# Attention and gated MLP in fp32 on one core: output weights of the last group in another place, matrix transposes for two block pairs instead of four, another order

## The chip, the cores and the metric

The kernel runs on one core of a Trainium2 chip. Its time is the device time of one execution in microseconds (us). TensorE is called PE here, VectorE DVE, ScalarE ACT, GpSimd POOL; SP is the engine whose queue issues nearly all DMAs.

## The reference

Two batches of 512 tokens with 512 features go through one post-normalised block, all in fp32:

```python
q, k, v = x @ Wq.T, x @ Wk.T, x @ Wv.T            # 32 query heads, 8 key/value heads of 128
q, k = rmsnorm(q) * q_norm_w, rmsnorm(k) * k_norm_w
scores = q @ k.T / sqrt(128) + slope[head] * (key_pos - query_pos)   # causal
x = layernorm(x + softmax(scores) @ v @ Wo.T)
h = silu((x @ gate.T) * gate_s) * ((x @ up.T) * up_s)                # int32 weights, 1376 wide
out = layernorm(x + (h @ down.T) * down_s)
```

## The kernel before

**Tiling.** A group is one key/value head with its four query heads; there are eight. A unit is a group, a batch and a block of 128 tokens, `(g, b, i)`; 64 units. Units go in pairs of neighbouring blocks, numbered 0 to 31: groups 0 to 5 for both batches each, then groups 6 and 7 for batch 0, then 6 and 7 for batch 1. Pair 0 is `(0, 0, 0..1)`, pair 1 is `(0, 0, 2..3)`, pairs 30 and 31 are `(7, 1, 0..1)` and `(7, 1, 2..3)`.

**Seven products.** Most matrix products are done as seven block products in place of eight (`seven`, `PLAN`). They need sums and differences of blocks of both factors, which DVE and POOL make ahead, partly in place: `sums_x` for the tokens (`sx`, and `xT` itself, one half of a batch at a time), `sums_q` for a group's q, k and v weights (`tq`), `sums_o` for its output weights (`to`). `project` does q, k and v of a pair so, except for pair 0, which `project_plain` does directly. Each product has a PSUM bank, named `pa`, `pb` or `pc`, which ACT or DVE empties into `c`. For groups 0 to 5 `project_out` applies the scheme twice, one inside the other, and needs a second level of sums, `ti`; for groups 6 and 7 (`g >= DEEP`) `project_pair` uses one level and no `ti`.

**A pair's way.** `heads` squares and sums q and k, takes the inverse root (a power on POOL, `inv`), scales into `sq`, and turns it so that features lie on partitions (`qT`, and `kT` with the key weights `kw`). There are two ways to turn a block. One: `nc.tensor.transpose` on PE into PSUM (`ptq`, `ptk`) and copies out. The other: DVE transposes squares of 32 x 32 (L1152), the result is written to DRAM in one DMA (`far_q`) and read back in another order (`qT<-far_q`), and ACT and POOL weigh the keys. `scores` multiplies by the keys (`sc`), adds the bias and takes the maximum on DVE, the exponential on ACT, and scales by the inverse sums. `attend` turns each 128 x 128 block of the result the same two ways: `pt` on PE, or DVE squares (`st`), a DMA to `far` and two DMAs back to `prT`. It then multiplies by the values (`pa` at L1370, `px` and `pz` at L1402). Which way a block goes is set by

```python
NEAR_Q = {(0, 0), (HKV - 1, 1)}
NEAR_P = {(0, 0), (HKV - 1, 1)}
```

as group and batch: pairs 0, 1, 30 and 31 use PE. The two ways leave the keys of a block in different orders, so the values of those pairs are put in the other order by DMA (`v`, `vs`), and the norm weights are kept in both orders (two columns of `qw` and `kw`).

**Output weights.** `load_o` brings a group's 1 MB into `wo`. There is one such buffer, so a load waits until the last product of the group before has read it. Groups 6 and 7 alternate, and each is loaded twice.

**Order.** Every piece of work is an entry of `Work` with a cost on each engine that may do it, a priority and its dependences. `Work.order` places the entries one after the other, always the one that can start first by these costs, and so picks engines, buffers and the order in each queue. A DMA counts there as its start plus 1.6, its size, and 0.6. `SHIFTS` is a list of seeds; each moves the priorities of the entries in a stretch at random before the order is made. On the chip each engine works through its own list in order and waits for semaphores.

**After the attention.** `norm1` normalises and transposes (`ptx`), `ffn_up` and `ffn_down` do the MLP.

Of the kernel before, what the change touches and what calls it, by code (L numbers as in the profile page):

```python
# [14 lines left out]
ALU = mybir.AluOpType  # L15
# [25 lines left out]
MAX_INIT = 3e38  # L41
NEAR_Q = {(0, 0), (HKV - 1, 1)}
NEAR_P = {(0, 0), (HKV - 1, 1)}
DEEP = HKV - 2
# [27 lines left out]
def pool_ts(n):  # L72
# [5 lines left out]
SHIFTS = (  # L78
    1000003, 1000006, 1000008, 1000014, 1000017, 1000025, 1000044, 1000058, 1000062, 1000075,
    1000109, 1000133, 1000283, 1000470, 1000520,  # L80
)
# [49 lines left out]
class Buf:  # L131


    def __init__(self, ring, name):
        self.ring, self.name = ring, name
        self.users = []
        self.home = None
        self.tile = None

    def make(self):  # L140
        ring, k = self.home
        self.tile = ring.pool.tile(
            ring.shape, ring.dtype, tag=f"{ring.name}{k}", name=self.name, bufs=1
        )

    def __getitem__(self, i):
# [3 lines left out]
class Work:  # L150
# [68 lines left out]
    def order(self):  # L219
# [43 lines left out]
        while ready:  # L263
            at_engine = {}
            for o in ready:
                t0 = room(o)
                if t0 is None:
                    continue
                for e, c in o["costs"].items():
                    s = max(t0, free.get("ACT" if e == "ACTQ" else e, 0.0))  # L270
                    if e == "POOL":
                        s = max(s, port["DVE"])
                    elif e == "DVE" and o["port"]:
                        s = max(s, port["POOL"])
                    at_engine.setdefault(e, []).append((s, o["prio"], s + c, o["n"], c))
            assert at_engine, "no work can start: " + ", ".join(
                b.name for o in ready for b in o["takes"]
            )
            best = None
            for e, found in at_engine.items():  # L280
                first = min(found)
                if best is None or first < best[0]:
                    best = (first, e)
            (s, _, _, n, c), e = best
            o = ops[n]
            ready.remove(o)
            if e == "ACT" and o["table"] and o["table"] != table[0]:
                table[0] = o["table"]
                c += TABLE
            o["eng"] = e  # L290
            if e in ("SP", "ACTQ"):
                free["ACT" if e == "ACTQ" else e] = s + o["issue"]
                dma = max(dma, s + 1.6) + c
                o["end"] = dma + 0.6
            elif e == "NONE":
                o["end"] = s
            else:
                free[e] = s + c
                o["end"] = s + c
                if e == "POOL" or (e == "DVE" and o["port"]):  # L300
                    port[e] = s + c
            o["start"] = s
            for b in o["takes"]:
                if b.home is None:
                    b.ring.take(b)
            for r in o["opens"]:
                r.open = True
            placed.append(o)
            for x in nexts[o["n"]]:
                left[x["n"]] -= 1  # L310
                if not left[x["n"]]:
                    x["at"] = at(x)
                    ready.append(x)
# [26 lines left out]
def post_ln_block(  # L340
# [53 lines left out]
    r_us = ring("all", "us", 1, [P, NF])  # L394
    r_qw = ring("all", "qw", 1, [P, 2])
    r_kw = ring("all", "kw", 1, [P, HKV + 1, 2])
    r_id = ring("all", "ident", 1, [P, P])
# [19 lines left out]
    r_kT = ring("att", "kT", 2, [P, S])  # L417
    r_v = ring("att", "v", 2, [P, NTB, HD])
    r_qT = ring("att", "qT", 2, [P, 2, NQ, (G + 1) * Q])
# [41 lines left out]

    w_qkv, w_o = {}, {}

# [52 lines left out]
    def load_o(g, prio):  # L516
        wo = Buf(r_wo, f"wo_{g}")
        w_o[g] = wo
        load(1.05, prio, lambda q: q.dma_start(wo.tile, wot[g]), [(wo, m) for m in range(4)])

# [249 lines left out]

    t_q, t_o, t_i = {}, {}, {}

    def sums_q(g, prio):
# [10 lines left out]
        )  # L784

    def sums_o(g, prio, after):

        t, w = Buf(r_to, f"to_{g}"), w_o[g]
        t_o[g] = t
        block = {(0, 1): 0, (0, 0): 1, (1, 1): 2, (1, 0): 3}  # L790
# [7 lines left out]
            after=after,  # L798
        )
        if g >= DEEP:  # L800
            return
# [14 lines left out]

    c_of, qTs, kTs, vs, v2s, prTs, aTs = {}, {}, {}, {}, {}, {}, {}

# [10 lines left out]
    def project_plain(p, prio):  # L829
# [5 lines left out]
        for (r, n), rg in zip([(0, 0), (0, 1), (1, 0), (1, 1)], (r_f, r_f, r_f, r_po)):  # L835
            banks[r, n] = Buf(rg, f"pp_{r}_{n}")
        for kc in range(NK):
# [122 lines left out]
    def heads(p, prio):  # L960
# [4 lines left out]
        if i == 0:  # L965
            kTs[g, b] = Buf(r_kT, f"kT_{g}_{b}")
            vs[g, b] = Buf(r_v, f"v_{g}_{b}")
        kT, v = kTs[g, b], vs[g, b]
        sq = Buf(r_sq, f"sq_{p}")
# [59 lines left out]
        for r in range(2):  # L1029

            def normed(e, r=r):
                if e == "ACT":
                    for h in range(G + 1):
                        nc.scalar.activation(  # L1034
                            sq[:, r, h, :],
                            c(r)[:, ts(h, HD)],
                            AF.Copy,
                            scale=inv[:, r, h : h + 1],
                        )
                    return  # L1040
                vec[e].tensor_tensor(
                    sq[:, r],
                    c(r)[:, : 5 * HD].rearrange("p (h d) -> p h d", h=G + 1),
                    inv[:, r].unsqueeze(2).to_broadcast([P, G + 1, HD]),
                    ALU.mult,
                )

# [8 lines left out]


        v2 = Buf(r_vs, f"vs_{p}")
        v2s[p] = v2
        if (g, b) in NEAR_P:  # L1060
            for m in range(NQ):
# [3 lines left out]
                    prio + 0.2,  # L1065
                    lambda q, m=m, at=at: q.dma_start(
                        v[ts(m, Q), i : i + 2, :], cb[at : at + H2 - 1 : 2, :, 1, 2 * HD :]
                    ),
                    [(v, (i + r, m)) for r in range(2)],
                    [(cb, (r, 1)) for r in range(2)],  # L1070
                )
            for m in range(2):
                load(
# [8 lines left out]
        else:  # L1082
            for r in range(2):
                copy_op(
                    HD,
                    prio + 0.2,
                    lambda r=r: v[:, i + r, :],
                    lambda r=r: c(r)[:, 5 * HD :],
                    [(cb, (r, 1))],
                    [(v, (i + r, m)) for m in range(NQ)],  # L1090
                    ("ACT", "POOL"),
                )
            copy_op(
# [6 lines left out]
                ("ACT", "POOL"),  # L1100
            )
        qT = qTs[p] = Buf(r_qT, f"qT_{p}")
        if (g, b) in NEAR_Q:
            for r in range(2):
# [23 lines left out]
            def evict_k(e):  # L1128
                dst = kT[:, i * P : (i + 2) * P].rearrange("p (m k r) -> p m k r", m=4, k=2)
                src = ptk[:, : 2 * P].rearrange("p (m r k) -> p m k r", m=4, k=2)  # L1130
                if e == "ACT":
                    nc.scalar.activation(dst, src, AF.Copy, scale=kw[:, g, 1:2])
                else:
                    nc.vector.tensor_scalar_mul(dst, src, kw[:, g, 1:2])

# [48 lines left out]
        for x in range(2):  # L1184

            def weigh(e, x=x):
                dst = kT[:, i * P : (i + 2) * P].rearrange("p (m k x c) -> p x m k c", k=2, x=2, c=Q // 2)
                src = qT[:, :, :, G * Q :].rearrange("p r (m x) (c k) -> p x (r m) k c", x=2, k=2)
                if e == "ACT":
                    nc.scalar.activation(dst[:, x], src[:, x], AF.Copy, scale=kw[:, g, 0:1])  # L1190
                else:
                    nc.gpsimd.tensor_scalar(
                        dst[:, x], src[:, x], kw[:, g, 0:1], 1.0, ALU.mult, ALU.mult
                    )
# [103 lines left out]
    def attend(u, prio):  # L1298
# [6 lines left out]
        key = f"{g}_{b}_{i}"  # L1305
        pr, v = pr_of[i], vs[g, b]
        p, r = divmod(units.index(u), 2)
        for j in range(i + 1):
            prT = prTs[u, j] = Buf(r_prT, f"prT_{key}_{j}")
# [5 lines left out]
            n = (NQ - a0) * Q  # L1315
            if (g, b) in NEAR_P:
                pt = Buf(r_po, f"pt_{key}_{j}")
# [80 lines left out]
        def halves(e):  # L1398
            for m, (q, j) in enumerate(both):
                prT = prTs[(g, b, j), j]  # L1400
                for k, (bank, val) in enumerate(zip(banks, (v[:, j, :], v2s[q].tile))):
                    nc.tensor.matmul(  # L1402
# [10 lines left out]
        for q, j in both:  # L1413
            reads += [(prTs[(g, b, j), j], m) for m in range(2)]
            reads += [(v, (j, m)) for m in range(NQ)] + [(v2s[q], m) for m in range(2)]
        W.add({"PE": 1.07}, prio + 0.4, halves, reads, [A(bank) for bank in banks])
# [358 lines left out]
    for p in range(NP):  # L1775
# [3 lines left out]
        if p > 0 and fresh:  # L1779
            load_qkv(g, u - 14.0)  # L1780
            load_o(g, u - 10.0)
        if p == 0:
            project_plain(p, u - 2.4)
        if fresh:
            sums_q(g, u - 3.0)
        if p > 0:
            if g == 0 or (g == 1 and b == 0 and i == 0):
                sums_x(b, i // 2, u - 3.0, lead if p > 1 else ())
            project(p, u - 2.4)
        heads(p, u - 1.8)  # L1790
# [412 lines left out]
```

## Time and profile before

| | |
|---|---|
| median of 3 runs | 970.32 us (969.92 to 971.77) |
| profiled execution | 973.81 us, its span 972.0 |
| granted PE clock, mean | 0.994 |
| PE busy | 98% of the span |
| DVE, POOL, ACT busy | 74%, 55%, 50% |
| DMA, mean | 152 GB/s, 147.71 MB in all |
| first matmul, end of the last | 1.3 us, 966.2 us after the span's start |

The profile is one execution. An instruction's row gives start and length; lengths of matrix instructions overlap, so the next may start before the one before has ended. An fp32 product of two 128-row tiles shows as two rows. Idle time stands with the instruction that came after it and with what ended it. The granted clock is the share of full speed that PE was given.

### The profile page before, as it was taken

The page shows a single profiled execution, that of the slowest core. Times are in us where ns is not written, and L with a number is a line of the kernel's source. Part 1 is how long each engine was busy: PE and PEld are TensorE (multiplying, and loading weights), DVE is VectorE, ACT ScalarE, POOL GpSimd, SP SyncE. Part 2 cuts the span into 40 slices and gives each one's busy share as a digit, 9 for nine tenths or more (in the row PEclk, how much of TensorE's full clock was granted, in tenths as well). Part 3 has the DMA queues.
Part 4 walks back from the last instruction along what each step waited for, and adds up shares of the span by engine and source line. Part 5 has one row for each costly group of instructions (what it writes and reads, how often), then busy time and mean ns, then how long its engine had stood idle before and what let it go on. Part 6 is the DMA issues. An engine that isn't in the chain of part 4 may idle for free.

```text
span 972.0 us, 14179 instructions
## 1 busy us (share of the span) xinstructions
PE 955.3 (98%) x4330; PEld 692.5 (71%) x4330; DVE 716.8 (74%) x1765; ACT 487.5 (50%) x1342; POOL 531.6 (55%) x592
## 2 busy tenths in 40 slices
PE   8999999999999999999999999999899999999997
PEld 5666766676767675766677666676677888888886
DVE  7666877878887878887777888776575666667644
ACT  2576475656555646556545656755354333333000
POOL 5666365659565837665777865967453432132120
PEclk9999999999999999999999999999899999999999
DMA  9133567756674847684746775865431233210001
GB/s 324 37 112 106 154 211 235 206 175 197 178 217 134 252 122 232 194 244 158 204 158 193 232 221 162 233 195 168 141 123 65 68 96 87 82 52 23 23 23 44
DMA packets 182797, 147.71 MB, mean 152 GB/s; under 512 B 26208, under 2 KB 166368, under 8 KB 181440
## 3 DMA queue, kind: packets, MB, share of 16 engines
q1 hardware_dynamic: 181856, 146.13, 49.2%
q8 instruction: 35, 0.57, 0.2%
q10 hardware_dynamic: 864, 0.66, 0.2%
q14 instruction: 42, 0.34, 0.1%
HBM read 92.62 MB, written 53.48 MB: 150 GB/s over the span
## 4 chain that ended last, share of the span: by engine, by line
PE 95%; DMA 3%; DVE 1%; SPq 0%; POOL 0%; issue 0%; POOLq 0%; DVEq 0%
PE pa_q L725 16%; PE sc L1227 12%; PE pa L1370 11%; PE pb_q L725 8%; PE pa_h L725 8%; PE pa_o L1594 8%; PE pb_h L725 4%; PE pb_o L1594 4%; PE pc_q L725 4%; PE pa_d L725 4%; PE pa_o L725 3%; PE pc_h L725 2%; PE pc_o L1594 2%; PE pb_d L725 2%; DMA wo<-in_wot_dram 2%; PE px L1402 2%
## 5 line engine op out<-in xcount | busy, mean ns | idle before, releaser
L1252 ACT ACTIVATE pr<-pr,nmax 128x48 f32<-128x48 f32 (+15 forms) x256 | 133.5, 522 | 97.3 <-DVE nmax L1236 95.8
L1227 PE MATMUL sc<-kT,qT 128*128 128x48 f32 (+15 forms) x512 | 153.3, 408 | 0.0
L1236 DVE CUSTOM_DVE_ANT_0 pr<-sc,bias 128x48 f32<-128x48 f32 (+15 forms) x256 | 110.2, 441 | 36.4 <-PE sc L1227 33.2
L1370 PE MATMUL pa<-prT,v 128*128 128x512 f32 (+1 forms) x320 | 135.9, 510 | 0.5 <-DMA prT<-far 0.4
L1227 PEld LDWEIGHTS sc<-kT,qT 128*128 128x128 f32 x512 | 86.9, 191 | 42.1 <-issue 19.2
L666 DVE TENSOR_TENSOR acc<-acc,pa_o 128x512 f32<-128x512 f32 (+2 forms) x128 | 72.7, 568 | 49.6 <-PE pa_o L1594 25.1
L1284 ACT ACTIVATE pr<-pr,rden 128x64 f32<-128x64 f32 (+12 forms) x213 | 92.3, 495 | 16.1 <-DVE rden L1267 15.9
L725 PE MATMUL pa_q<-tq,sx 128*128 128x384 f32 x248 | 90.2, 487 | 0.0
L942 DVE STREAM_TRANSPOSE st<-pr 128x512 f32<-128x512 f32 (+1 forms) x140 | 84.0, 634 | 2.4 <-POOL pr L1286 1.3
L652 POOL TENSOR_TENSOR inv<-ms,nhalf 128x10 f32<-128x10 f32 (+1 forms) x33 | 65.7, 1992 | 22.1 <-DVE ms L1014 20.8
L1370 PEld LDWEIGHTS pa<-prT,v 128*128 128x128 f32 x320 | 55.3, 191 | 22.3 <-issue 5.0
L822 ACT COPY gu<-pa_h 128x256 f32<-128x256 f32 (+1 forms) x88 | 32.1, 370 | 77.5 <-PE pa_h L725 63.3
L725 PEld LDWEIGHTS pa_q<-tq,sx 128*128 128x128 f32 x248 | 46.0, 190 | 29.9 <-issue 7.5
L822 ACT COPY c<-pa_q 128x384 f32<-128x384 f32 x78 | 37.1, 476 | 57.8 <-PE pa_q L725 49.0
L977 ACT ACTIVATE sq<-c 128x640 f32<-128x640 f32 x64 | 45.2, 730 | 32.0 <-DVE c L1152 23.4
L1034 ACT ACTIVATE sq<-c,inv 128x128 f32<-128x128 f32 x160 | 50.1, 389 | 14.6 <-POOL inv L652 14.6
L1286 POOL TENSOR_SCALAR pr<-pr,rden 128x64 f32<-128x64 f32 (+10 forms) x75 | 34.8, 475 | 37.4 <-DVE rden L1267 37.2
L666 POOL TENSOR_TENSOR si<-so 128x384 f32<-128x384 f32 x21 | 21.0, 1001 | 59.1 <-PE pb_o L1594 57.1
L1000 DVE TENSOR_REDUCE ms<-sq 128x5 f32<-128x640 f32 x64 | 51.1, 811 | 0.5 <-ACT sq L977 0.5
L1152 DVE STREAM_TRANSPOSE c<-sq 128x320 f32<-128x320 f32 x112 | 50.7, 485 | 0.0
L1594 PEld LDWEIGHTS pa_o<-ti,si 128*128 128x128 f32 x336 | 42.9, 192 | 8.1 <-issue 2.9
L1252 ACT ACTIVATION_READ_ACCUMULATOR pr<-pr,nmax 128x1 f32 x256 | 48.0, 188 | 0.0
(238 smaller groups left out, 2242.7 us busy)
## 6 DMA issues: line engine op xcount, KB each, us to landing
far<-st SPq DMA_DIRECT2D x112, 256.0 KB, 2.9
prT<-far SPq DMA_DIRECT2D x224, 128.0 KB, 3.1
far_q<-c SPq DMA_DIRECT2D x28, 640.0 KB, 3.8
qT<-far_q SPq DMA_DIRECT2D x56, 320.0 KB, 3.8
w<-in_wqkv_dram SPq DMA_DIRECT2D x39, 384.0 KB, 4.9
wo<-in_wot_dram SPq DMA_DIRECT2D x10, 1024.0 KB, 7.1
far<-st SPq DMA_DIRECT2D x28, 128.0 KB, 2.5
prT<-far SPq DMA_DIRECT2D x56, 64.0 KB, 2.8
```

Source lines behind the costliest of these rows:

```text
L652: lambda e: nc.gpsimd.tensor_tensor(dst(), src(), nhalf[:, :n], ALU.pow),
L666: lambda e: vec[e].tensor_tensor(dst(), a(), b(), alu),
L725: nc.tensor.matmul(bank[:rows, :width], lhsT=a(fa, c), rhs=b(fb, c), start=(fresh and c == 0), stop=(c == depth - 1), skip_group_check=True,)
L822: nc.scalar.copy(dst(), src())
L942: {"DVE": dve(n)}, prio, lambda e: nc.vector.transpose(dst(), src()), reads, [A(st)]
L1000: lambda e, r=r: nc.vector.tensor_reduce(ms[:, r], sq[:, r], AX.X, ALU.add),
L1227: lambda e, a=a, w=w, sc=sc: nc.tensor.matmul(sc[:, :w], lhsT=qT[:, r, a, : G * Q], rhs=kT[:, :w], start=True, stop=True),
L1236: lambda e, a=a, w=w, sc=sc: nc.vector.tensor_tensor_reduce(out=pr[:, a, :w], in0=sc[:, :w], in1=bias[:, S - w :], scale=-(SHRINK**-g), sc ...
L1252: lambda e, a=a, w=w: nc.scalar.activation(pr[:, a, :w], pr[:, a, :w], AF.Exp, bias=nmax[:, a : a + 1], scale=-1.0, accum_out=den[:, a : a ...
L1284: nc.scalar.activation(dst, src, AF.Copy, scale=rden[:, a : a + 1])
L1370: lambda e, j=j, prT=prT, n=n: nc.tensor.matmul(by_head(po.tile)[:, :, P - n // G :], lhsT=v[:, j, :], rhs=late(prT, j, n), start=(j == 0) ...
L1594: nc.tensor.matmul(bank[:, ts(c, P)], lhsT=a(fa, c), rhs=b(fb, c), start=fresh and c == 0, stop=True, skip_group_check=True,)
```

## The change

1. `load_o` for the last group takes its buffer from the ring of `ti` (seen through `view` in the shape of `wo`), after everything that used `ti` for groups 0 to 5. Group 6 keeps the buffer of `wo`. The first step of each `sums_o` also waits for the last of the one before.
2. `NEAR = {0, 31}` replaces the two sets: pairs 0 and 31 alone turn blocks on PE. Pairs 1 and 30 go by DRAM. For the near pairs the normalisation writes the features in the order that the other way gives, so `qw` and `kw` keep one column. A pair's values are kept in the order that each later pair of its group and batch will need: in `vn` by DMA, in `v` by copies, or in both (for pairs 0 and 30). The ring of `v` has three buffers.
3. A DMA's start counts as 2.0 in the planner, and there are other seeds. The order changes throughout.

```diff
-NEAR_Q = {(0, 0), (HKV - 1, 1)}
-NEAR_P = {(0, 0), (HKV - 1, 1)}
+NEAR = {0, 31}
+PLAIN = 1
...
 SHIFTS = (
-    1000003, 1000006, 1000008, 1000014, 1000017, 1000025, 1000044, 1000058, 1000062, 1000075,
-    1000109, 1000133, 1000283, 1000470, 1000520,
+    22000003, 22000016, 22000019, 22000030, 22000031, 22000059, 22000062, 22000085, 22000096,
+    22000110, 22000180, 22000208, 22000219, 22000282, 22000333, 22000351, 22000369, 22000431,
+    22000607, 22000642,
 )
...
-                dma = max(dma, s + 1.6) + c
+                dma = max(dma, s + 2.0) + c
...
-    r_v = ring("att", "v", 2, [P, NTB, HD])
+    r_v = ring("att", "v", 3, [P, NTB, HD])
...
     def load_o(g, prio):
-        wo = Buf(r_wo, f"wo_{g}")
+        if g == HKV - 1:
+
+            flat = lambda t: t.rearrange("p j n c -> p (j n c)")[:, : 4 * DM]
+            view = lambda t: flat(t).rearrange("p (m k c) -> p m k c", m=4, k=2)
+            wo = Buf(r_ti, f"wo_{g}", view)
+            after = [o for t in t_i.values() for o in t.users]
+        else:
+            after = []
+            wo = Buf(r_wo, f"wo_{g}")
         w_o[g] = wo
-        load(1.05, prio, lambda q: q.dma_start(wo.tile, wot[g]), [(wo, m) for m in range(4)])
+        load(1.05, prio, lambda q: q.dma_start(wo[:, :], wot[g]), [(wo, m) for m in range(4)], after=after)
...
         t, w = Buf(r_to, f"to_{g}"), w_o[g]
+
+        after = after + [last_sums[-1]] if last_sums else after
...
             def normed(e, r=r):
+                dst = sq[:, r]
+                src = c(r)[:, : 5 * HD].rearrange("p (h d) -> p h d", h=G + 1)
+                if p in NEAR:
+                    dst = dst.rearrange("p h (r m) -> p h m r", m=NQ)
+                    src = src.rearrange("p h (m r) -> p h m r", m=NQ)
...
-        if (g, b) in NEAR_P:
+        users = [q for q in range(NP) if pairs[q][:2] == (g, b) and pairs[q][2] >= i]
+        if any(q in NEAR for q in users):
+            if (g, b) not in vns:
+                vns[g, b] = Buf(r_v, f"vn_{g}_{b}")
+            vn = vns[g, b]
...
+        if any(q not in NEAR for q in users):
+            if (g, b) not in vs:
+                vs[g, b] = Buf(r_v, f"v_{g}_{b}")
+            v = vs[g, b]
...
-        if (g, b) in NEAR_Q:
+        if p in NEAR:
...
-            if (g, b) in NEAR_P:
+            if p in NEAR:
...
-        if p == 0:
+        if p < PLAIN:
             project_plain(p, u - 2.4)
```

## The prediction

> **What bounds the kernel now.** I read the page first: one engine is busy nearly throughout.
>
> ```profile
> PE 955.3 (98%) x4330; PEld 692.5 (71%) x4330; DVE 716.8 (74%) x1765; ACT 487.5 (50%) x1342; POOL 531.6 (55%) x592
> ```
>
> So a microsecond counts if it is TensorE (PE) work or a place where PE stands still. The timeline of PE, searched for holes, gives nearly all of the second kind. Columns: start, length, engine, line, operation, count, and in brackets the idle time before it with what ended it.
>
> ```profile
> 20.83 1.21 PE L1109 MATMUL ptq<-ident,sq 128*128 128x128 f32 x4 [2.83 <-ACT sq L1034]
> 22.01 0.78 PE L1124 MATMUL ptk<-ident,sq 128*128 128x128 f32 x2
> 23.24 2.88 PE L725 MATMUL pb_q<-w,xT 128*128 128x384 f32 x4 [0.46 <-DVE xT L666]
> ```
> ```profile
> 664.97 0.89 PE L725 MATMUL pa_o<-wo,aT 128*128 128x256 f32 x3 [2.40 <-DMA wo<-in_wot_dram]
> ...
> 695.60 2.08 PE L725 MATMUL pa_o<-wo,aT 128*128 128x256 f32 x4 [2.51 <-DMA wo<-in_wot_dram]
> 697.47 1.91 PE L725 MATMUL pc_o<-wo,aT 128*128 128x256 f32 x4
> ```
>
> The other holes are 0.15, 0.17, 0.24 and 0.62 us, together 1.2, besides 1.34 at the start. The third and last reading is the windows view over the same places (length, busy time of PE, PEld, DVE, ACT and POOL, then granted clock, DMA share, GB/s):
>
> ```profile
> 24.00:26.00 2.00, 2.00 (x5) 0.97 (x4) 1.81 (x5) 0.00 (x0) 0.62 (x1) 0.51 0.96 350
> 666.00:668.00 2.00, 2.00 (x11) 1.77 (x10) 1.65 (x4) 0.00 (x0) 2.00 (x3) 1.00 0.17 21
> 699.00:700.00 1.00, 1.00 (x3) 0.76 (x3) 0.42 (x1) 0.00 (x0) 0.92 (x2) 0.50 0.89 272
> ```
>
> After the holes at 18 and 693 PE runs at half clock for some us; after the one at 662 it does not. So I price a hole by its whole stretch. From 18.00 to 25.94 PE did six transposes and one product: 6 x 0.109 + 1.29 = 1.94 us at full clock, so 6.0 are lost. From 662.40 to 664.97 2.6 are lost. From 692.94 to 701.74 it did 14 matmuls of 0.216 = 3.0, so 5.8 are lost, 2.66 of them standing.
>
> **The change, part by part.** *Fewer transposes on PE.* They go for pair 1 (units (0,0,2), (0,0,3)) and pair 30 ((7,1,0), (7,1,1)). Pair 1: 8 for q, 2 for k, 2+4+4 and 4x4 for the attention blocks, 36; pair 30: 10 and 2+4+4, 20. Together 56; the built program has 2190 matrix instructions against 2246, and no other difference on PE. The price is the step from one to the next, not the length shown:
>
> ```profile
> 45.10 0.60 PE L1109 MATMUL ptq<-ident,sq 128*128 128x128 f32 x4
> 45.54 1.46 PE L725 MATMUL pc_q<-w,xT 128*128 128x384 f32 x4
> ```
>
> Four take 45.54 - 45.10 = 0.44, so 0.109 each and 56 x 0.109 = **6.1 us** less. [...]
>
> In their place come 28 more DMAs on SP (642 to 670: 12 more writes to DRAM, 24 more reads, 8 fewer value copies), near 0.6 us of issue each, and on VectorE (DVE) 18 more block transposes of 0.49 to 0.68 against some copies of 0.69. SP, and DVE at 74%, have the room, except where PE has nothing else to do: at the start. Eight more small copies of values on ACT and POOL (0.28 to 0.31 each), the one-column norm weights and the reordered normalisation lie under PE work too; with no cover at all they would cost 8 x 0.3 = 2.4 us.
>
> *Output weights.* Both holes at 662 and 693 are a 1 MB load that can start only when the group before is done with the one buffer:
>
> ```profile
> 656.61 8.22 DMA wo<-in_wot_dram
> ...
> 687.15 8.40 DMA wo<-in_wot_dram
> ```
>
> With two places, group 7's load starts when the sums of group 5 are done. I price the built order of PE by the trace's steps (0.216 us a record of 256 columns, two records a matmul, others in proportion). Counted so, the second load for group 6 has 30 us between release and need, group 7's second 36. These 5.8 and 2.6 go. What is late next is the first load for group 6: released at 630.0 of PE work, needed at 639.1, and group 7's load sits three SP rows ahead of it (from 627.4), with score blocks queued behind both. 9.1 us were just enough before (6.6 of work plus 2.6 of hole). The loads take 4.7 to 8.8 us to land, median 7.1; two one after the other at 8.2 would land at 644 (4.9 late), but the windows view has 246 to 279 GB/s while the first of them ran (659 to 662) and 360 to 401 in the second (689 to 691), and 2.3 MB at 280 take 8.2 us from 628.9, so 637 (0 late). I take 1.0, nearer to the rates. Gain 8.4 - 1.0 = **7.4**.
>
> *The start.* All of it is reordered. PE now has seven products (1.29 each) instead of two between pair 0's projection, which ends at 15.42, and its transposes, so it reaches those at 24.45. With the durations of the old rows in the new order, what they need comes in time. DVE: eight key weights of 0.31 from 10.7, bias 0.65, w's sum 0.95 to 14.8; then 0.45, 0.95 and 0.45 to xT's sum at 16.6. POOL's sum of 1.05 follows, to 17.7. DVE's two reductions of 0.81 end at 19.1, POOL's bias row and last sum at 20.3, its two powers of 1.2 at 22.7, and DVE's normalisation of 0.83 at 23.6. The first hole closes: -6.0. But pair 1's round trip now fills the same engines. By my count PE is through the attention of unit (0,0,1) at 42.8: since 15.42 it has done 16 products of 1.29, 20 transposes (2.2), eight score matmuls (2.3) and the value matmuls (1.7), 26.9, and waited 0.5 for a copy. Next comes the product pb_q of pair 3, which needs the sum of xT's second half. On DVE that sum now stands behind pair 1's four transposes (they wait for ACT to 40.6, end 42.5), an add of 0.55, pair 2's two reductions of 0.81 (ACT's squares end at 45.0) and a small add: done at 46.9. In the old order PE had transposes to do here. So PE stands **4.1 us**. The clock after it: 2.57 us of standing cost nothing more, 2.66 cost 3.1, 2.83 cost 2.7; I take 2.2 between 0 and 3.4. Together 0.5 + 4.1 + 2.2 = 6.8 lost against 6.0: **-0.8**. Pair 1's keys then come in time (51.4 against a need at 53.4 or later).
>
> [...]
>
> *Other shifts.* They reorder every stage. Tight places are alike (least PE work from a unit's last score to its first value matmul: 11.4 before, 11.1 after). I put the small holes at 2.0 for 1.2: **-0.8**, between 0 and 5.
>
> Sum: 6.1 + 7.4 - 0.8 - 0.8 = **11.9 us**. The profiled execution took 973.81 (span 972.0 plus 1.8 around it), so 961.9 there. The median of the runs is 970.32, 3.5 lower: 958.4.
>
> **Rivals.** *Slower: the block round trip outlasts its cover.* From pair 3 on, PE work between a pair's projection and its first scores was 24.5 us for pair 3 and over 34 for all others; now it is 27.2 (pair 3), 29.2 (4), 30.0 (8), 28.3 (20), 30.6 (21), 31.2 (25), 31.9 (29), 32.3 (27). In the trace pair 3 needed 22.5 us until its keys were ready, pair 2, with weight loads in the queue, 30.1. If all need X, PE waits X minus each of these: 12.5 us in sum at X = 31.5, which eats the gain, about 23 at 33, giving 981. Against it: in the trace most keys are ready only 0.1 to 3 us before their scores and PE does not wait, so the order tracks the chip closely, and it now counts 0.4 us more for each DMA. 0.08.
>
> *The weight hole moves to the first load of group 6* at full size, 4.9 and half clock after it, 3: the gain falls by 7, to 965. For it: two loads in one queue. Against: the packet rates. 0.15.
>
> *The start stays dense*, if DVE and ACT run ahead of my walk by 4 us: 6.8 less, 952. The walk rests on some forty rows, but each wait in it is a real dependence. 0.12.
>
> **Numbers.** Forecast 958.4, chance 0.62; 0.03 for anything else. The low end is the forecast with the head hole 2 us long and clock kept, and no weight wait (953). The high end leaves room for what the median's 3.5 us below the profile hints, that half-clock stretches are shorter in other runs (3 us less to gain), and 3 to 4 more of small holes or most of the weight rival: 966. A measurement of this kernel can tell about 0.2%, 1.9 us. Faster than that 0.88, within it 0.04, slower 0.08.
>
> **What would show it.** Right: 4274 PE instructions or nearly; no PE wait on wo over 1 us; clock 1.00 at 690 to 705; no hole at 18; a hole of 3 to 5 us near 43, ended by DVE on xT or sx, half clock after it. Wrong: PE waiting for qT or prT from DRAM in several later pairs, or holes elsewhere adding up to over 5 us.

## The result and the profile after

| | before | after |
|---|---|---|
| median of 7 runs beside each other | 970.38 us (968.56 to 972.12) | 966.36 us (961.54 to 966.80) |
| ratio of the times | | 0.9949, 95% interval 0.9930 to 0.9968 |
| profiled execution | 973.81 us | 966.59 us |
| PE's first matmul to the end of its last | 1.3 to 966.2 us | 1.3 to 958.7 us |

The changed kernel is faster by 4.0 us; the forecast was 11.9, to 958.4. All runs that stood beside others together give 970.57 (99 runs of the kernel before, 966.3 to 975.0) and 966.16 (25 runs of the changed one, 961.5 to 969.9): 4.4 us.

The page after, the line of the engines. PE has the 56 matrix instructions less that were foreseen; its share has not moved.

```profile
PE 946.9 (98%) x4274; PEld 684.9 (71%) x4274; DVE 724.6 (75%) x1791; ACT 482.9 (50%) x1343; POOL 516.8 (54%) x587
```

The timeline of PE, searched for holes as before. Columns: start, length, engine, line, operation, count, and in brackets the idle time before it with what ended it.

```profile
46.47 2.93 PE L736 MATMUL pb_q<-w,xT 128*128 128x384 f32 x4 [3.43 <-DVE xT L677]
134.28 0.48 PE L1429 MATMUL pz<-prT,vs 64*128 64x256 f32 x1 [0.55 <-ACT aT L837]
136.18 1.32 PE L1252 MATMUL sc<-kT,qT 128*128 128x304 f32 x4 [0.78 <-ACT kT L1215]
...
261.77 1.10 PE L1397 MATMUL pa<-prT,v 128*128 128x512 f32 x2 [0.60 <-DMA prT<-far]
...
661.31 1.10 PE L736 MATMUL pa_o<-wo,aT 128*128 128x256 f32 x4 [0.47 <-DVE c L1177]
698.00 1.10 PE L1397 MATMUL pa<-prT,v 128*128 128x512 f32 x2 [1.24 <-DMA prT<-far]
867.81 1.10 PE L736 MATMUL pb_h<-x1T,sw 128*96 128x256 f32 x4 [1.55 <-DVE gu L677]
```

The hole that was foreseen at the start is there, ended by the row that was named. The two holes that waited for output weights have shrunk to one of 0.47 (the profile names a DVE row there, which had long ended; POOL's sum of `wo` waits until the same 661.3, and for the load). But at 697 stands a new wait for a block transfer, and there are small holes all along that the kernel before did not have.

The windows view (length, busy time of PE, PEld, DVE, ACT and POOL, granted clock, DMA share, GB/s) shows half clock behind the hole at the start and full clock where the kernel before had the other stretch of it:

```profile
47.00:49.00 2.00, 2.00 (x4) 1.01 (x3) 0.73 (x1) 0.73 (x3) 1.24 (x1) 0.50 0.61 156
...
699.00:701.00 2.00, 2.00 (x9) 1.39 (x8) 0.89 (x5) 0.34 (x2) 0.00 (x0) 1.00 0.59 182
```

### The profile page after: what moved, and what is told of

Read it like the earlier page. It is cut to its first block, busy times and chain, and to the rows that moved or that the text cites. A ratio compares the mean times of both kernels' runs of the same rounds, so it can differ in the third digit from the quotient of the medians.

```text
span 964.8 us, 14143 instructions
## 1 busy us (share of the span) xinstructions
PE 946.9 (98%) x4274; PEld 684.9 (71%) x4274; DVE 724.6 (75%) x1791; ACT 482.9 (50%) x1343; POOL 516.8 (54%) x587
## 4 chain that ended last, share of the span: by engine, by line
PE 91%; DMA 4%; DVE 3%; issue 1%; SPq 0%; ACT 0%; ACTq 0%; POOLq 0%; DVEq 0%; POOL 0%
PE pa_q L736 16%; PE sc L1252 13%; PE pa L1397 11%; PE pa_h L736 8%; PE pb_q L736 8%; PE pa_o L1621 7%; PE pb_h L736 4%; PE pc_q L736 4%; PE pb_o L1621 4%; PE pa_d L736 4%; PE pa_o L736 2%; DMA prT<-far 2%; PE pc_h L736 2%; PE pc_o L1621 2%; PE pb_d L736 2%; PE px L1429 2%
## 5 line engine op out<-in xcount | busy, mean ns | idle before, releaser
L1252 PE MATMUL sc<-kT,qT 128*128 128x176 f32 (+15 forms) x512 | 153.0, 408 | 0.9 <-ACT kT L1215 0.8
L1397 PE MATMUL pa<-prT,v 128*128 128x512 f32 (+1 forms) x300 | 126.3, 510 | 2.5 <-DMA prT<-far 2.5
L1309 ACT ACTIVATE pr<-pr,rden 128x256 f32<-128x256 f32 (+11 forms) x200 | 85.7, 491 | 20.9 <-DVE rden L1292 20.6
L957 DVE STREAM_TRANSPOSE st<-pr 128x512 f32<-128x512 f32 (+1 forms) x150 | 90.4, 635 | 5.7 <-ACT pr L1309 2.5
L837 ACT COPY c<-pa_q 128x384 f32<-128x384 f32 x85 | 40.4, 476 | 79.0 <-PE pa_q L736 72.4
L1397 PEld LDWEIGHTS pa<-prT,v 128*128 128x128 f32 x300 | 53.3, 191 | 26.7 <-issue 5.6
L1311 POOL TENSOR_SCALAR pr<-pr,rden 128x64 f32<-128x64 f32 (+10 forms) x88 | 41.5, 484 | 50.5 <-DVE rden L1292 50.2
L1054 ACT ACTIVATE sq<-c,inv 128x128 f32<-128x128 f32 x170 | 53.4, 396 | 17.2 <-POOL inv L663 17.0
L1177 DVE STREAM_TRANSPOSE c<-sq 128x320 f32<-128x320 f32 x120 | 54.8, 487 | 0.1
L736 PE MATMUL pb_q<-w,xT 128*128 128x384 f32 x124 | 47.1, 503 | 3.4 <-DVE xT L677 3.4
```

The source lines that it names most:

```text
L736: nc.tensor.matmul(bank[:rows, :width], lhsT=a(fa, c), rhs=b(fb, c), start=(fresh and c == 0), stop=(c == depth - 1), skip_group_check=True,)
L837: nc.scalar.copy(dst(), src())
L957: {"DVE": dve(n)}, prio, lambda e: nc.vector.transpose(dst(), src()), reads, [A(st)]
L1177: lambda e, r=r, m=m: nc.vector.transpose(cb[:, m] .rearrange("p n w -> p (n w)")[:, :half] .rearrange("p (m r h d) -> p r h m d", m=2, r= ...
L1252: lambda e, a=a, w=w, sc=sc: nc.tensor.matmul(sc[:, :w], lhsT=qT[:, r, a, : G * Q], rhs=kT[:, :w], start=True, stop=True),
L1309: nc.scalar.activation(dst, src, AF.Copy, scale=rden[:, a : a + 1])
```

## The experiments

Two kinds of kernel were run. In one the planner makes a new order. In the other the order stays, and single entries are moved in it, which keeps all else in place:

```diff
-        for o in self.order():
+        placed = self.order()
+        for n, at in [...]:            # each run's list: entry n goes right behind entry at
+            placed.remove(self.ops[n])
+            placed.insert(placed.index(self.ops[at]) + 1, self.ops[n])
+        for o in placed:
```

Each run is named by its edit. Times are medians; ratios are against the kernel before, run beside it. Differences to the changed kernel go against the 966.16 of all its runs; its three medians lie between 964.87 and 967.28, so such a difference is good to 1 to 2 us.

**Is one profile enough? The kernel before once more** (`again`, no edit).

> The kernel before, unchanged. Theory (the half clock differs from run to run): its profiled execution lost about 5.8 us to half clock (mean clock 0.994 of 972.0) and its ordinary runs less; then the runs here show a mean clock that goes up as the time goes down, near 0.996 to 0.997 at 970, and some run near 973 with 0.994. Rival (the profile itself costs 3.5 us): all runs of one clock, 0.994, at 970.4, and only the profiled one near 973.8. The change's own profiled execution, no slower than its other runs, speaks against the rival.

971.26 us (12 runs); its profiled execution took 970.97. The same holes in its timeline of PE:

```profile
21.39 1.35 PE L1109 MATMUL ptq<-ident,sq 128*128 128x128 f32 x4 [2.48 <-ACT sq L1034]
23.80 2.90 PE L725 MATMUL pb_q<-w,xT 128*128 128x384 f32 x4 [0.37 <-DVE xT L666]
663.64 1.10 PE L725 MATMUL pa_o<-wo,aT 128*128 128x256 f32 x4 [0.26 <-DMA wo<-in_wot_dram]
693.75 1.13 PE L725 MATMUL pa_o<-wo,aT 128*128 128x256 f32 x4 [1.98 <-DMA wo<-in_wot_dram]
704.49 1.10 PE L1370 MATMUL pa<-prT,v 128*128 128x512 f32 x2 [1.84 <-DMA prT<-far]
```

The two holes that wait for an engine come again nearly alike (2.83 as 2.48, 0.46 as 0.37). Those that wait for a transfer do not: 2.40 has become 0.26, 2.51 has become 1.98 with no half clock behind it, and a wait for `prT` of 1.84 has come in. The rival falls (the profile costs nothing), and the theory holds in part: mean clocks lie between 0.993 and 0.997 in these runs, but they do not order the times well. The execution that I priced everything from was itself a slow one, 3.2 us over the median of 99.

**The weights alone** (`wo_alone`): the kernel before, its order kept; group 7's buffers go to the ring of `ti`, its loads and group 6's second go behind the last use of their new place.

```diff
+        for n in (3345, 3873):         # the first and second load of group 7
+            wo = self.ops[n]["takes"][0]
+            wo.ring, wo.home, wo.view = self.ti, (self.ti, 0), self.view
```

> The kernel before in its own order on every engine, and group 7's output weights alone put where the second level's sums lay; the three loads that this frees are issued as soon as their place is free. Theory of the prediction's term: both holes (2.4 and 2.5 us standing) and the half clock after the second go, 8.4 us of the profiled execution (973.8 to 965.4), and as much of the median if the half clock comes in each run: 962. Rival: in most runs of before the second hole does not drop the clock, so that only the standing time goes, 5 us: 965.4. Third: the transfers freed early collide with the others and give back 1 to 2 us: 967.

971.82 us; ratio 1.0012 (0.9999 to 1.0025): nothing gained. Its timeline of PE has no wait for `wo` in it, and these:

```profile
673.21 1.32 PE L1240 MATMUL sc<-kT,qT 128*128 128x304 f32 x4 [1.56 <-ACT kT L1203]
...
703.88 1.31 PE L1383 MATMUL pa<-prT,v 128*128 128x512 f32 x2 [2.14 <-DMA prT<-far]
```

The chain of waits (start, length, what) shows what each stood behind. For the first:

```profile
657.80 9.18 DMA far_q<-c
...
668.80 3.63 DMA qT<-far_q
672.43 0.02 issue
672.45 0.72 ACT kT L1203 x2
...
673.21 1.32 PE sc L1240 x4
```

For the second, SP issues DMAs one behind the other from 696.3 on, four of them copies of pair 31's values (L1079), before it comes to the block's (L1360):

```profile
698.65 0.61 SPq L1079
...
699.31 0.60 SPq L1079
699.91 0.05 issue
700.01 0.60 SPq L1360
700.66 3.09 DMA prT<-far
703.75 0.14 issue
703.88 1.31 PE pa L1383 x2
```

So the waits for `wo` had stood in front of others that were late as well, and the edit made one of them worse: it issues group 7's load at 656.70, right behind group 6's at 656.11 and ahead of this `far_q`. 4.2 us of standing between 650 and 710 here, 4.1 in `again`.

**The reloads left out** (`wo_skip`): the order before; group 7's two loads and group 6's second are not issued, so that the sums use other weights than the reference's. Group 6's first load stays.

```diff
+            if any(o is x for x in skip):
+                o["takes"][0].tile = kept.tile
+                continue
```

> The kernel before in its own order, with the last three loads of output weights left out: groups 7, 6 and 7 then use the place and what the sums left in it, so the result is not the reference's, while all other work, the sums among it, stays. Theory of the prediction's term: without the waits for these loads 5 us of standing and 3 of half clock go, 962. Rival A (what stands behind them in the same stretch is late as well: the round trips of keys and attention blocks through DRAM): holes of 1 to 2 us at 670 to 705 that wait for prT or kT, and 968 to 970. Rival B (the loads' traffic makes those round trips late): no such holes, and the gain is whole, 962 to 964.

967.51 us; ratio 0.9968 (0.9955 to 0.9981), 3 us. Its timeline of PE between 650 and 710 has one hole over 0.2:

```profile
700.37 1.10 PE L1375 MATMUL pa<-prT,v 128*128 128x512 f32 x2 [0.65 <-DMA prT<-far]
```

By its holes rival B is nearest, by its time rival A. The traffic explains only a part. The hole at 662 waited for group 6's first load, which is issued here too (656.67), so that its absence is a draw, like 2.40 and 0.26 in the two profiles of the kernel before. Pair 29's `far_q` stands behind that same load and landed in 5.8 us, against 6.6 in `again`, 9.1 in the first profile of before, and 9.2 behind two loads in `wo_alone`. Only from 686 on is a load missing. The whole of what the three loads cost is 3 us at the median, not 8.

**The weights put back in the changed kernel** (`wo_back`): its own order; the three loads go behind the last use of the one buffer.

> The changed kernel in its own order, with group 7's output weights back in the one buffer: its two loads and group 6's second go behind the last product of the group before, as they stood in the kernel before. Theory of the prediction's term: the holes come back at 672 to 700 and 725, each 2.5 us or more, with half clock after the longest: 7 to 8 us, 964.9 to 966.4 plus 7.4 is 972 to 974. Rival (the loads and the block transfers share the transfer engines, so that what is gained on one is lost on the other): +3 or less, as the run without the reloads gained, 966 to 969.

978.42 us, ratio 1.0084 (1.0064 to 1.0103): 12 us lost (11 against `after_third`, run beside it), more than the theory's 7.4. The timeline of PE, and the chain of waits at the longer hole:

```profile
691.48 1.10 PE L744 MATMUL pa_o<-wo,aT 128*128 128x256 f32 x4 [3.33 <-DMA wo<-in_wot_dram]
...
721.69 1.19 PE L1405 MATMUL pa<-prT,v 128*128 128x256 f32 x2 [3.92 <-DMA prT<-far]
```
```profile
714.57 0.88 PE pb_o L744 x4
715.44 0.02 SPq L538
715.47 0.03 issue
715.50 0.35 SPq L538
715.85 0.05 issue
715.90 5.66 DMA prT<-far
```

SP waits at the load (L538) until PE has done with the buffer at 715.4; the block's transfer is issued behind it and lands in 5.66, where the medians of such reads were 2.9 and 2.6 (128 and 64 KB, from 655 to 706). Half clock comes with both holes: the granted clock was 0.63 from 692 to 694 and 0.52 from 694 to 696, and 0.50 from 720 to 722 and from 724 to 726. So the price of a load that waits in SP's queue hangs on what needs it and on what is queued behind it: 3 us in one order, 12 in another. This order was made for two places and I put the loads in by hand; that one planned for one place would be better is likely, but no run shows it.

**The transposes alone** (`pe56`): the changed kernel's order; 28 idle transposes ahead of a product of pair 12, 28 ahead of one of pair 20.

```diff
+                if name in ("q12", "q20") and k == "b" and fresh:
+                    for _ in range(28):
+                        nc.tensor.transpose(bank[:, :P], ident.tile, ident.tile)
```

> The changed kernel in its own order with 56 idle transposes put back on PE, 28 ahead of one product of pair 12 and 28 ahead of one of pair 20, where the profile shows PE dense. Theory: each costs its step, 0.109, and nothing else moves: +6.1 us, 964.9 to 966.4 before it, so 971 to 972.5. Rival (work on PE gives the transfers behind it time, so that later waits shrink by as much as they can): +4 or less, 969 to 970.

972.41 us, 6.2 over the changed kernel's 966.16 of all runs (5.1 to 7.5 over its three medians). In the profile the added transposes follow each other every 0.109 us, and 56 x 0.109 = 6.1 holds. It also says that without these 56 the change would be no faster than the kernel before (ratio of this run 1.0016, 0.9995 to 1.0037).

**All transposes back, planned anew** (`near4`): `NEAR = {0, 1, 30, 31}`.

> The changed kernel with the 56 transposes back on TensorE (pairs 0, 1, 30 and 31), planned anew. Theory: PE has 56 x 0.109 = 6.1 us more to do, and the hole near 43 (3.4 and up to 3.4 of half clock) goes, since pair 1 needs no round trip, but a hole near 18 of 2.5 to 2.8 may come back: 966.4 + 6.1 - 1 (0 to 6) = 968 to 972. Rival (the transposes lie where PE would stand anyway): 965 to 967.

989.90 us, ratio 1.0190, far outside both expectations. Of some 24 us, 6 are the transposes. The waits of PE in its list of waits (us, times, longest) are those of a bad order:

```profile
PE pa L1397 <- DMA prT<-far: 4.6, 4, 3.8
PE sc L1252 <- DVE nmax L1261: 4.1, 3, 2.4
PE pt L1348 <- ACT pr L1309: 2.0, 1, 2.0
```

It stands 20.4 us in all against 10 to 12 in the changed kernel, and the granted clock is 0.50 from 566 to 568, from 570 to 572 and from 728 to 730 (mean 0.988). The same seeds move the same priorities, but around other work.

**The shifts alone**, both ways: the changed kernel with the old seeds and 1.6 (`oldseeds`), and the kernel before with 19 of the new seeds and 2.0 (`newseeds_b`).

> The changed kernel planned with the old shifts and the old 1.6 us in place of 2.0; NEAR and the place of group 7's weights stay new. Theory of the prediction (shifts move small holes, 1 to 5 us): 964.9 to 966.4 plus 0 to 5, at most 971. Rival (the shifts are fitted to one structure, and an unfitted order costs as much as the 56 transposes that came back with a new plan did beyond their 6.1 us, some 17): 978 to 985.

970.13 us: 4.0 over 966.16, within what was expected, at its upper end. This prices the seeds and not the forecast's term, which set the new order against that of the kernel before. Against that kernel the ratio is 0.9986 (0.9967 to 1.0005): with the old seeds the other parts of the change gain nothing clear.

> The kernel before, planned with 19 of the 20 new shifts (with all of them its plan has no end) and with 2.0 us in place of 1.6, its transposes and its weights as before. Theory of the prediction: 970.4 plus 0 to 5. Rival (unfitted order): 980 to 990, with holes of 1 us and more that wait for prT, qT or kT, and the half clock behind them.

974.63 us, 3.9 over its own structure. Each structure loses 4 us with the other's seeds: they are part of the change as much as its other parts, and what either set is worth hangs on the work it is used for.

**The hole at the start filled** (`fill`): 28 idle transposes ahead of the product that waits at 43.

> The changed kernel with 28 idle transposes (28 x 0.109 = 3.05 us) ahead of the product that waits near 43, so that PE is busy there though nothing comes sooner. Theory: the hole's price is 3.4 us of standing, which stays, and 3.4 us from half clock in the 6.8 us after it, which goes: 966.4 - 3.4 = 963.0, clock 0.998 or over. Rival: the half clock has another cause or what follows waits for VectorE anyway, so nothing is gained: 966.4.

966.26 us: nothing gained at the median, though the clock did what the theory says (mean 0.999 in the profile, no half clock before PE's end). In its profile two waits for transfers have grown that were 0.60 and 0.21 in the changed kernel's:

```profile
258.90 1.10 PE L1402 MATMUL pa<-prT,v 128*128 128x512 f32 x2 [1.86 <-DMA prT<-far]
```
```profile
655.56 1.12 PE L1402 MATMUL pa<-prT,v 128*128 128x512 f32 x2 [1.90 <-DMA prT<-far]
```

Eight runs from 961.5 to 968.2 leave open how much of this is chance.

**The hole at the start closed.** First try (`head5`): xT_1's three second-half sums go ahead on DVE, two products of pair 3 ahead of pair 1's scores. Those two products now come ahead of copies that they should follow, so that a part of pair 3's projection is summed from other values; the run is read for its waits.

> The changed kernel in its own order but for five steps: xT_1's second-half sum goes ahead on VectorE to where it has room (36.4), the two sums after it to 43.5, and two products of pair 3 go ahead of pair 1's first scores. Theory: the hole of 3.4 us and the 3.4 us of half clock both go, pair 1's keys (whole at 54.2 in the profile, by VectorE and ScalarE that are then earlier) come by the first scores at 52.0 or cost under 1 us: 966.4 - 6 = 960. Rival: the hole only moves on, to pair 1's keys (2 us) or to pair 2's chain, whose DMAs do not come sooner: 963 to 966.

966.78 us: the hole moved on. The product behind next stood 2.42 us for a copy on ACT, which stood in ACT's queue behind pair 2's normalisation, which waits for POOL's power:

```profile
50.83 1.91 PE L740 MATMUL pa_q<-tq,sx 128*128 128x384 f32 x4 [2.42 <-ACT c L841]
```

Second try (`head6`): the three sums as before, both copies on ACT ahead of that normalisation, and the first of those two products ahead of pair 1's scores, behind its copy.

> The changed kernel in its own order but for the steps at the start of the run named best alone. Theory: the hole near 43 and its half clock are worth what the prediction priced, 6.8, less what is left at 49 to 50 (0.8): 964.9 to 966.4 less 4 to 6 is 960 to 962. Rival (the gain of best came as much from its two late steps): 963 to 965.

962.36 us, ratio 0.9914 (0.9894 to 0.9934): the hole and its half clock were worth 4 to 5 us (3.8 by all runs of the changed kernel, 4.9 by `after_third`, run beside it). One run of seven, the profiled one, took 968.16: there PE, now earlier, stood for the first load of group 6, with half clock behind it (the product at 663.39 took 2.56 to the next row in place of 1.29).

```profile
661.23 1.10 PE L740 MATMUL pa_o<-wo,aT 128*128 128x256 f32 x4 [2.03 <-DMA wo<-in_wot_dram]
```

**Two late steps** (`late`): group 7's first load goes behind the six block transfers that it stood in front of; at 865 DVE's drain of `pb_h` goes ahead of the product for `hT`.

> The changed kernel in its own order but for two steps: group 7's first load goes behind the six block transfers that it stood in front of (SP, 648), and near 865 VectorE's drain of pb_h goes ahead of the product for hT that it waited behind (1.55 us of PE standing at 866). Theory: the hole at 866 goes or shrinks to under 0.4 (-1.2 to -1.5), and those at 657 and 661 lose 0.3 to 2: 964.5. Rival: the drain's place is taken by the next wait on VectorE and the load comes too late for group 7 (needed at 688): 966.4.

964.10 us (5 runs), against 964.87 of the changed kernel beside it: unclear. The hole at 866 went from 1.55 to 0.95, no wait for `wo` was left.

**Both together** (`best`).

> The changed kernel in its own order but for both steps of the run named late, and at the start: xT_1's three second-half sums go ahead on VectorE, and pair 3's and pair 4's copies on ScalarE go ahead of pair 2's normalisation, so that neither waits for the other. Theory: the hole at 43 (3.4) and half clock after it (3.4) shrink to what pair 1's keys or POOL's sums of w leave, 1 to 3 us: 964.1 - 3 = 961. Rival (the start is bound by VectorE and POOL, whose work is the same): the standing moves on to the product that waits for POOL's sum of group 1's weights near 61, 3 us or more: 963 to 965.

960.48 us (959.77 to 963.67), ratio 0.9890 (0.9870 to 0.9910): faster than both kernels. The theory holds. Its page and its timeline of PE, where the start's hole stood:

```profile
PE 945.2 (99%) x4274; PEld 683.0 (71%) x4274; DVE 723.6 (75%) x1791; ACT 482.3 (50%) x1343; POOL 518.2 (54%) x587
```
```profile
50.62 1.56 PE L740 MATMUL pa_q<-tq,xT 128*128 128x384 f32 x4 [0.76 <-ACT c L841]
```

**The changed kernel again**, twice.

> The changed kernel, unchanged. Theory (one execution of either kernel is a draw): the spread of single runs is 3 us or more to either side, as the kernel before showed (966.3 to 973.8 in 31 runs), the holes at 43 (3.4) and 866 (1.6) come again to 0.2 us, those that wait for a transfer (165, 261, 657, 661, 697; 3.0 together) do not. Median 966 +- 1. Rival (the holes are fixed by the order): all of them within 0.3 us of the first profile.

964.87 us (963.47 to 965.71); ratio 0.9935 (0.9916 to 0.9953).

> The changed kernel once more, on the chip of the two runs beside it, so that they stand against it: 964.9 to 966.4, with the hole of 3.4 near 43 in its profile and 3.4 to 6.8 us of half clock behind it. If its median lies outside, the differences of under 2 us told so far are those of chips and not of kernels.

967.28 us (964.32 to 969.88); ratio 0.9966 (0.9950 to 0.9981). The holes at 43 (3.42, 3.43) and 866 (1.55, 1.55) came again to 0.01. Those for `prT` in the three profiles: 0.46, 0.67, 0.74 near 165, 0.60, 0 and 0.88 near 262, 1.24, 1.14, 1.13 near 697. Its median lies outside what was expected: between jobs, on different chips, the changed kernel differs by up to 2.4 us (the kernel before gave 970.33 to 970.73 in all four), so a difference of 1 to 2 us is read only between runs of one job.

## Why the prediction was wrong in size and right in direction

The five profiles of the two kernels allow an account that closes. Standing is read from the timeline. Half clock is taken to cost half the time that PE works in it (the product of 1.29 us took 2.70 at 23.24 before). Work is PE's end less both and less the first 1.3.

| us | before, 1st profile | before, `again` | after, 1st | `after_again` | `after_third` |
|---|---|---|---|---|---|
| own time | 973.81 | 970.97 | 966.59 | 964.71 | 967.15 |
| end of PE | 966.2 | 963.3 | 958.7 | 956.8 | 959.3 |
| work | 950.7 | 950.8 | 944.1 | 945.0 | 945.3 |
| standing to 60, without the first 1.3 | 3.4 | 2.9 | 4.2 | 3.7 | 3.7 |
| standing from 650 to 710 | 4.9 | 4.1 | 2.1 | 1.4 | 2.5 |
| standing elsewhere | 1.3 | 1.3 | 4.1 | 3.7 | 4.8 |
| lost to half clock | 4.6 | 3.0 | 2.8 | 1.7 | 1.7 |

**Fewer transposes, 6.1 us: right.** The work fell by 6.0 (950.8 to a mean of 944.8), and `pe56` gives 6.2 for the same number.

**Output weights, 7.4 us: this is the step that failed.** The loads do wait less, as foreseen; the size was not as foreseen. From `again`, which lies near the median, to the changed kernel's three profiles the standing from 650 to 710 fell by 2.1 (4.1 to a mean of 2.0), and there was no half clock there to lose (in `again` the granted clock was 1.00 in each 10 us from 655 to 705). Two things were wrong in the step. The 8.4 was the price of one execution: both holes wait for transfers, and these differ from run to run (2.40 against 0.26). And to my own question, what is late next, I answered with the first load of group 6 alone. It was the blocks' and keys' round trips (`wo_alone`), and the most that was had by leaving the loads out was 3 us (`wo_skip`).

The largest wait of the stretch in the changed kernel shows how a load that is moved takes the place of the one that is gone. The chain that ends at the hole near 697:

```profile
686.92 7.41 DMA far<-st
...
694.35 0.60 SPq L1374
...
695.00 2.87 DMA prT<-far
...
698.00 1.10 PE pa L1397 x2
```

The write of the blocks to `far` is issued behind group 6's second load, which the second place lets go at 685.21; in `again` that load went at 716.13. The median of such writes between 655 and 706 is 2.6 us; this one took 7.41, 7.29 and 7.28 in the three profiles, each time 1.7 us behind that load, and the hole was 1.24, 1.14 and 1.13. With the write at 2.6 SP would come to the read near 693.4, behind its copies of values, in place of 694.35, so that some 0.3 of the 1.24 would be left, by estimate; no run moved this load alone.

The first load of group 6, my 1.0, was late by 0.5, under 0.2 and 0.7 in three profiles, near enough; it came to 2.0 when PE got there sooner (`head6`). It keeps its buffer, so it is the new order and not the second place that gave it more time.

**The start, 0.8 us lost: right.** Standing rose by 1.0 and half clock fell by 0.9 from `again`. I had PE standing 4.1 from 42.8 to 46.9; it was 3.4, from 43.05 to 46.47, ended by the sum on DVE that was named. The 2.2 for the clock after it, between 0 and 3.4, was in these three profiles 2.8, 1.7 and 1.7. One of the figures that the 2.2 came from was misread: of the 2.7 behind the 2.83 us hole only some 1.5 was clock. The trace has full clock until 22.56, and the six transposes before that came every 0.29 us at full clock. `best` shows the hole's price from the other side: with the sums and copies in another place it is gone.

**Other shifts, 0.8 us lost: mis-sized.** Standing elsewhere rose from 1.3 to a mean of 4.2, by 2.9, within the 0 to 5 that I had given but not near the value I took. I chose it by the tightest places of one kind alone, from scores to values. Two of the new holes come in each profile and wait for engines, not for transfers: `pb_h` at 866 (1.55) and `pz` at 134 (0.54 to 0.55).

**From the profile to the median, 3.5 us: failed.** I took the same difference off the forecast. The changed kernel's three profiled executions lie within 0.3 us of the medians beside them; the first one of before lay 3.2 over. Part of what made it long was the very thing that the change was to remove, so that the gain was counted from a bad draw. I had written that half clock may be shorter in other runs and gave it 3 us of the range; that is what came. This is not lost on top of the weights' term: it is one reason why that term was too large.

From `again`: -6.0 work, -2.1 weights, +0.1 start, +2.9 elsewhere make -5.1. The medians say -4.4. Had the terms been so, the forecast would have been 970.3 - 5.1 = 965.2.

**The rivals.** The block round trip did outlast its cover, at 135, by 0.78, under 0.2 and 0.67 in three profiles: 0.8 us and not 12. The first load of group 6 was late, at a tenth of what that rival gave it; the figure of that rival, 965, lies near the median by luck, for its mechanism is not what took the gain. The start did not stay dense.

## What to carry to other kernels

Price a hole from more than one profile, above all one that waits for a transfer: here the waits for an engine came again to 0.35 us in the kernel before and to 0.01 in the changed one, while a wait for the same load was 2.40 and 0.26. Before counting a closed stall as gained, list every other transfer on the same queue that is due soon after (`wo_alone` closed holes at 662 and 693, and PE stood at 672 and 702), and what is issued right behind a load that moves; here one of them took its place. Where a hole ends on an engine's queue, look at what stands ahead of the late instruction there: a handful of entries moved by hand (`head6`, 3.8 us) gave nearly as much as the whole change.

## What the runs showed of the hardware

The granted clock stood at 0.50 from 22.56 to 25.97 and from 694.98 to 701.81 in the first profile of the kernel before, and from 45.29 to 52.11 in that of the changed one: for 3.41, 6.83 and 6.82 us. The same hole drew different lengths. Standing of 3.42 to 3.43 us near 43 was followed by those 6.82 us in the changed kernel's first profile and by 3.4 in `after_third` (0.55 from 48 to 50, 0.60 from 50 to 52, full clock on both sides). From the start of each of the two products behind the hole to the next row it took, where 1.29 is full pace:

| us | after, 1st | `after_again` | `after_third` | `pe56` | `wo_back` | `late` |
|---|---|---|---|---|---|---|
| first product | 2.73 | 2.31 | 1.71 | 2.73 | 2.20 | 1.39 |
| second product | 2.56 | 2.06 | 2.56 | 2.55 | 2.18 | 1.29 |

So in `late` 3.43 us of standing drew none, while a hole of 2.48 in `again` did draw half clock (0.74 from 20 to 22, 0.50 from 24 to 26, 0.55 from 26 to 28). The length of a hole alone did not decide it here, and what does was not shown.

On DVE a product of two operands in SBUF took 2.02 us in one place of the changed kernel, with POOL at work beside it, and 0.73 in another. The timeline of DVE near the hole at 866, and that of POOL at the same time:

```profile
858.88 0.73 DVE L1994 SCALAR_TENSOR_TENSOR hT<-gu,us_sb,sg 128x512 f32<-128x512 f32 x1
...
865.07 2.02 DVE L1994 SCALAR_TENSOR_TENSOR hT<-gu,us_sb,sg 96x512 f32<-96x512 f32 x1
```
```profile
864.83 1.71 POOL L677 TENSOR_TENSOR sh<-hT 128x640 f32<-128x640 f32 x1
```

The first ran while POOL was idle, the second beside POOL's product for 1.47 of its 2.02, and the drain that PE waited for at 866 stood behind it. Not each overlap did so: at 880.48 the product took 0.75 with a sum of 1.17 on POOL beside it from 880.64 on. No run here moves POOL's product away, so that the cause is only argued.
